# First stage of a four-layer convolution kernel: group norm by half-pair units with VectorE transposes in place of TensorE matmuls

## The chip, the cores and the metric

The kernel runs on one core of a Trainium2 chip. The metric is device time in microseconds (us) of one execution. Five engines work beside each other, each through its own fixed list of instructions: TensorE (PE in the profile, its weight loads PEld), VectorE (DVE), ScalarE (ACT), GpSimd (POOL) and SyncE (SP), which here only issues DMA transfers. ScalarE and GpSimd issue a few transfers too.

## What is computed

The input x has 8 images of 384 channels with 32 x 32 pixels. Four layers follow one another, each of the form x = x + layer(groupnorm(x)). Only the first matters here, and of it the part up to its batch norms:

```python
def _gn(v, G=32, eps=1e-5):
    g = v.reshape(B_, G, C_ // G, H_, W_)
    m = jnp.mean(g, axis=(2, 3, 4), keepdims=True)
    s = jnp.var(g, axis=(2, 3, 4), keepdims=True)
    return ((g - m) / jnp.sqrt(s + eps)).reshape(v.shape)

def _dwproj(x, dw, g, b, pw):          # for q, k and v
    y = lax.conv_general_dilated(x, dw, (1, 1), ((1, 1), (1, 1)), feature_group_count=C, ...)
    y = jax.nn.gelu(_bn(y, g, b), approximate=False)
    return jnp.einsum('oc,bchw->bohw', pw, y)

x = x + _L0_conv_ref(_gn(x), ...)      # q, k, v by _dwproj, attention in 8 heads, projection, batch norm
```

Each image is normalised over groups of 12 channels. Three depthwise 3 x 3 convolutions, for q, k and v, read the normalised image. Each result gets a batch norm, whose mean and variance run over all 8 images, then a gelu and a 384 x 384 product. So no result of the convolutions can be used until the statistics of all images are there: the convolved values go to device memory and are fetched again in the next stage.

## The kernel before, in words

The whole first stage is written out by hand: a manual schedule holds every engine to the order of the program text.

**Stacks.** The input was laid out on the host as `xs`. A stack puts the four image rows that two neighbouring output rows read on four neighbouring partitions (partition modulo 4 is the row offset d; d = 0 and 3 are rows of the neighbours, so each image row lies twice). A tile `xs` m holds half an image (two of its four channel sets g, three channel chunks c each, 512 columns per chunk) in 128 x 3072 values, loaded by four transfers of 384 KB (L281), one for each d. Before, `load_half` makes tile m of image m // 2, half m % 2. There are 16 tiles; eight are loaded at the start, the first four by SP and ScalarE together. Some tiles live in five image buffers that later stages use too, the others in a pool of six.

**Work.** Images are taken in pairs k = 0 to 3. Each pair has ten works: four of kind y (first chunk of q, k and v together), four of kind a (a later chunk of q and k), two of kind v (a later chunk of v). A work is a run of small matmuls (L545) into four PSUM banks, alternating between the `big` and the `mm` pool; then copies by ScalarE into a tile y (L555, two of 1024 columns or four of 512), four of 512-column statistics by VectorE (L561), and four stores by SP to device memory (L566, L571, L580; 128 or 256 KB each). The pool of y has four buffers. In the last pair VectorE also aggregates the statistics (L585).

**Norm.** `norm(k)` gives the steps that normalise pair k, and the table AT says at which work of pair k-1 each of them is put into the engines' order:
- `begin`, four times: VectorE takes statistics of a tile (six L334, two L337).
- `middle`: TensorE multiplies the means and variances by the group matrix `gs4` (L343, into bank `gpa`); VectorE copies (L348), subtracts (L351) and squares (L352).
- `end`: a second matmul by `gs4` (L358, `gpb`), VectorE adds (L360), GpSimd takes the power -0.5 (L98), VectorE makes the shift (L365).
- `apply`, four times: ScalarE scales and shifts 128 x 1536 values of each image (L379; for the second image of pair 0 VectorE does it, L377), and GpSimd zeroes the rows outside the image (four L382).

For pair 0 all of it stands ahead of the first work. For pairs 1 and 2 AT is (0, 0, 1, 2, 4, 5, 6, 7, 8, 9). The loads of later tiles are queued on SP between the stores, two or four parts per work.

**End of the stage.** Ahead of the last pair's stores SP moves the tile statistics of x (L486, eight small transfers). Ahead of the last-but-one work, `spread_qk` begins to spread q's and k's statistics, with two matmuls behind that work (L425); it borrows one y buffer. Behind that work's copies ScalarE applies the gelus of q and k of image 0 (L243). After the last work `spread_v` does the same for v with one matmul (L458, `pmovev`). Then the next stage begins on TensorE with the projection `pq` (L703).

Of the kernel before, what the change touches and what calls it, by code (L numbers as in the profile page):

```python
# [14 lines left out]
P = 128  # L15
# [40 lines left out]
def tile_kernel(ctx: ExitStack, tc: tile.TileContext, i: dict, out: bass.AP):  # L56
# [199 lines left out]
    with ExitStack() as pa:  # L256
# [8 lines left out]
        halves_of = {}  # L265
        IN_IM = (0, 1, 2, 3, 4, 11, 12)

        def load_half(m, queue):

            b, h = divmod(m, 2)  # L270
            t = (
                image(f"xs{m}") if m in IN_IM
                else xa.tile([P, KC, N], F32, tag="xs", name=f"xs{m}")
            )
            halves_of[m] = t.rearrange("p c n -> p (c n)").rearrange("p (k n) -> p k n", n=HALF)

            def part(d):
                w = KC * N
                s = W + (0 if d in (1, 2) else W if d == 3 else -W)
                src = i["xs"][s : s + B * C * N].rearrange("(b e m n) -> b e m n", b=B, e=2, m=32)  # L280
                queue[d].dma_start(  # L281
                    out=t.rearrange("p c n -> p (c n)")[d::4],
                    in_=src[b, 1 - d % 2, :, h * w : (h + 1) * w],
                )

            return [lambda d=d: part(d) for d in range(4)]

        for m in range(4):
            for f in load_half(m, (nc.sync, nc.sync, nc.scalar, nc.scalar)):
                f()  # L290
        gs4 = wa.tile([P, P], F32, name="gs4_sb")
        nc.gpsimd.dma_start(out=gs4, in_=i["gs4"])
# [5 lines left out]
        for m in range(4, 8):  # L298
            for f in load_half(m, 4 * (nc.sync,)):
                f()  # L300
        g4 = const.tile([P, P], F32, name="g4_sb")
        ident = const.tile([P, P], F32, name="ident_sb")
        sels = wa.tile([P, 3, P], F32, name="sels_sb")
        isv = wa.tile([P, 5], F32, name="isv_sb")
        msk = wa.tile([P, 28], F32, name="msk_sb")
# [12 lines left out]
        sv = wa.tile([P, KC - 1, 4, NK, 6], F32, name="sv")  # L318
        zy = wa.tile([P, 16, 2], F32, name="zy")
        zqk = wa.tile([P, KC - 1, 8, 2], F32, name="zqk")  # L320
        zv = wa.tile([P, KC - 1, 4, 2], F32, name="zv")
# [3 lines left out]
        def norm(k):  # L325

            state = {}
            mv = sa.tile([P, 2, 4, 2], F32, tag="gp_mv", name=f"gmv{k}")
            xt = [[halves_of[4 * k + 2 * j + h] for h in range(2)] for j in range(2)]

            def begin(j, h):
                for g in (2 * h, 2 * h + 1):
                    for c in range(KC):
                        nc.vector.bn_stats(  # L334
                            xst[:, g, 2 * k + j, c, :], xt[j][h][:, g % 2 * KC + c, :]
                        )
                    nc.vector.bn_aggr(  # L337
                        mv[:, j, g, :], xst[:, g, 2 * k + j].rearrange("p c s -> p (c s)")
                    )

            def middle():
                pg = bank(f"gpa{k}")
                nc.tensor.matmul(  # L343
                    pg[:, :16], lhsT=gs4, rhs=mv.rearrange("p j g s -> p (j g s)"),
                    start=True, stop=True,
                )
                ga = sa.tile([P, 8, 2], F32, tag="gp_ga", name=f"gga{k}")
                nc.vector.tensor_copy(ga.rearrange("p j s -> p (j s)"), pg[:, :16])  # L348
                dm = sa.tile([P, 8], F32, tag="gp_dm", name=f"gdm{k}")
                mvf = mv.rearrange("p j g s -> p (j g) s")  # L350
                nc.vector.tensor_tensor(dm, mvf[:, :, 0], ga[:, :, 0], ALU.subtract)  # L351
                nc.vector.tensor_tensor(dm, dm, dm, ALU.mult)  # L352
                state["ga"], state["dm"] = ga, dm

            def end():
                ga, dm = state["ga"], state["dm"]
                pb = bank(f"gpb{k}")
                nc.tensor.matmul(pb[:, :8], lhsT=gs4, rhs=dm, start=True, stop=True)  # L358
                ve = sa.tile([P, 8], F32, tag="gp_ve", name=f"gve{k}")
                nc.vector.scalar_tensor_tensor(  # L360
                    ve, pb[:, :8], 1e-5, ga[:, :, 1], ALU.add, ALU.add
                )
                ss = sa.tile([P, 2, 8], F32, tag="gp_ss", name=f"gss{k}")
                rsqrt(ss[:, 0, :], ve, 8)
                nc.vector.scalar_tensor_tensor(  # L365
                    ss[:, 1, :], ga[:, :, 0], -1.0, ss[:, 0, :], ALU.mult, ALU.mult
                )
                state["ss"] = ss

            def apply(g):  # L370
                ss, h = state["ss"], g // 2
                for j in range(2):
                    n = 4 * j + g
                    d = xt[j][h][:, g % 2 * KC : g % 2 * KC + KC, :]
                    sc, sh = ss[:, 0, n : n + 1], ss[:, 1, n : n + 1]
                    if k == 0 and j == 1:
# [9 lines left out]

            return (
                [lambda j=j, h=h: begin(j, h) for j in range(2) for h in range(2)]
                + [middle, end] + [lambda g=g: apply(g) for g in range(4)]
            )  # L390

        PLAN = ["y0 a01 y1 a11 y2 v1 y3 a02 a12 v2"] * last + [
            "y0 a01 y1 a11 y2 a02 y3 a12 v1 v2"
        ]
        work = [
            (k, w[0], int(w[1]), int(w[2:] or 0)) for k, p in enumerate(PLAN) for w in p.split()
        ]
        NW = len(work) // NK
        AT = (0, 0, 1, 2, 4, 5, 6, 7, 8, 9), (0, 3, 3, 4, 6, 7, 8, 8, 9, 9)
        steps = {}  # L400

        def spread_qk():
# [9 lines left out]
            for z, n, dst in zip(zs, nv, both):  # L412
                sq = sa.tile([P, ng], F32, tag="ssq", name=f"ssq{n}")
                nc.vector.tensor_tensor(sq, z[:, :, 0], z[:, :, 0], ALU.mult)
                nc.vector.tensor_tensor(z[:, :, 1], z[:, :, 1], sq, ALU.add)
                for s in range(2):
                    nc.vector.tensor_tensor(
                        dst[:, :, s], z[:, :, s].unsqueeze(1).to_broadcast([P, n, ng]),
                        isv[:, v0 : v0 + n].unsqueeze(2).to_broadcast([P, n, ng]), ALU.mult,
                    )  # L420
# [29 lines left out]

        def spread_v():

            m = zv.rearrange("p c g s -> p (c g) s")
            sq = sa.tile([P, 8], F32, tag="ssv", name="ssv")
            nc.vector.tensor_tensor(sq, m[:, :, 0], m[:, :, 0], ALU.mult)
            nc.vector.tensor_tensor(m[:, :, 1], m[:, :, 1], sq, ALU.add)
            pm = bank("pmovev")
            nc.tensor.matmul(  # L458
                pm[:, :16].rearrange("p (s x) -> p s x", s=2), lhsT=sels[:, 2, :],
                rhs=m.rearrange("p x s -> p s x"), start=True, stop=True,  # L460
            )
            got = sa.tile([P, 4, 4], F32, tag="gotv", name="gotv")
            nc.vector.tensor_tensor(
                got, pm[:, :16].rearrange("p (x g) -> p x g", g=4),
                msk[:, 24:].unsqueeze(1).to_broadcast([P, 4, 4]), ALU.mult,
# [3 lines left out]
            nc.vector.tensor_copy(fv[:, :, 1:], f.rearrange("p (s c) -> p s c", s=2))  # L469
# [25 lines left out]
        for n, (k, kind, s, c) in enumerate(work):  # L495
            at = n % NW
            if kind == "v":
                c = s
            if at == 0:
                for m in ((8, 9, 10, 11), (12,), (13, 14, 15), ())[k]:  # L500
                    loads += load_half(m, 4 * (nc.sync,))
                if k == 0:
                    load_late()
                steps = {}
                for a, f in zip(AT[k + 2 > last], norm(k + 1) if k < last else ()):
                    steps.setdefault(a, []).append(f)
            for _ in range(2 if k == 0 else 4):
                if loads and (k > 0 or at > 1):
                    loads.pop(0)()
            if k == last - 1 and at == 3:  # L510
                acts[0] = {v: image(f"g{v}_0") for v in (2, 1, 0)}
                for v, t in acts[0].items():
                    loads += fetch_raw(t, v, rqk[0], rv[:, 0])
            if k == last and at == 0:
# [3 lines left out]
            if k == last and at == 8:  # L518
# [5 lines left out]
            else:  # L524
                two = [big(f"pk{n}_{r}") for r in range(2)]
                banks = [two[r // 2][:, r % 2 * HALF : (r % 2 + 1) * HALF] for r in range(4)]
                outs = [(t, 2 * r, 2) for r, t in enumerate(two)]
            passes = [(j, x) for j in range(2 if kind == "v" else 1) for x in (1, 0, 2)]
            nq = 2 if kind == "y" else 4
            cols = [slice(P // nq * q, P // nq * (q + 1)) for q in range(nq)]  # L530
            for p in passes:
                j, x = p
                c0, c1 = max(0, 1 - x), W - max(0, x - 1)
                for q in range(nq):
                    if kind == "v":
                        g, w = q, slice(32 + 16 * j, 64 + 16 * j)
                    elif kind == "y":
                        g, j, w = s, q, slice(0, 64)
                    else:
                        (u, j), w = divmod(q, 2), slice(0, 32)  # L540
                        g = 2 * s + u
                    src = halves_of[4 * k + 2 * j + g // 2][:, g % 2 * KC + c, :]
                    src = src.rearrange("p (h w) -> p h w", w=W)
                    for r, rs in enumerate(quads):
                        nc.tensor.matmul(  # L545
                            banks[r][cols[q]].rearrange("p (h w) -> p h w", w=W)[:, :, c0:c1],
                            lhsT=cws[rs, c, g, x, w], rhs=src[rs, :, c0 + x - 1 : c1 + x - 1],
                            start=(p == passes[0]), stop=(p == passes[-1]),
                        )
            if k == last and at == 8:  # L550
# [3 lines left out]
            for src, r, w in outs:  # L554
                nc.scalar.copy(y[:, r : r + w, :].rearrange("p a n -> p (a n)"), src)  # L555
            st = (
                sy[:, 4 * s : 4 * s + 4] if kind == "y"
                else sv[:, c - 1] if kind == "v" else sqk[:, c - 1, s]
# [3 lines left out]
            for q in range(4):  # L562
                if kind == "y":
                    v, j = divmod(q, 2)
                    to = rqk[2 * k + j, c] if v == 0 else rv[c, 2 * k + j]
                    nc.sync.dma_start(  # L566
                        out=to[:, 4 * s : 4 * s + 4, :],
# [1574 lines left out]
```

## Time and profile before

| what | us |
| --- | --- |
| runs: median of 3 (lowest to highest) | 3538.39 (3537.48 to 3539.07) |
| the profiled execution's own time | 3538.58 |
| its span in the profile | 3536.8 |
| TensorE busy (share of the span) | 3386.1 (96%) |
| VectorE, ScalarE, GpSimd busy | 1686.8, 1294.6, 213.8 |
| first matmul of the convolutions L545 / first of the next stage L703 | 35.56 / 269.18 |
| matmuls of the convolutions L545, busy in all | 178.2 |
| VectorE statistics of the tiles L334, mean of one | 0.67 |
| VectorE statistics of y L561, mean of one | 0.68 |
| ScalarE applications L379, mean of one | 1.70 |

A row of the order of time has start, length, engine, line, operation, tile written <- tile read, shape, the count of instructions merged in it, and in brackets how long the engine was idle before and what ended the wait. A row of a stretch has its bounds and length, then busy time and instruction counts of PE, PEld, DVE, ACT and POOL, the granted TensorE clock (1.00 is full), the busy share of the 16 DMA engines and GB/s. The median of the runs and the profiled execution differ by 0.2 us.

### The profile page before, as it was taken

The numbers are of one execution on the slowest core, as the hardware profiler recorded it, in microseconds if no ns is written. First come the engines' busy times: TensorE is split into PE (matmuls) and PEld (weight loads), VectorE is DVE, ScalarE is ACT, GpSimd is POOL, SyncE is SP. The second block draws the span as 40 slices with busy tenths as digits, with TensorE's granted clock in tenths as the row PEclk, the third lists the DMA queues.
The fourth block names the chain that finished last, engine by engine and source line by source line (L and its number), as shares of the span: only waits on it lengthen the run. The fifth ranks groups of instructions, "written<-read, shape, count | busy, mean of one in ns | idle before, by whom it ended". The sixth has DMA issues, their size and how long they took to land.

```text
span 3536.8 us, 44871 instructions
## 1 busy us (share of the span) xinstructions
PE 3386.1 (96%) x18615; PEld 1459.1 (41%) x18615; DVE 1686.8 (48%) x2821; ACT 1294.6 (37%) x1512; POOL 213.8 (6%) x226
## 2 busy tenths in 40 slices
PE   5879999999999999998999999999999999999897
PEld 2333434343434343433344444444444444434434
DVE  6762232323232323234256475564755647556663
ACT  3554544444444444433212323223232232332222
POOL 2100000000000000000000100101001010010112
PEclk9999999999999999999999999999999999999898
DMA  8883212121212121121800010101101011010000
GB/s 301 245 256 85 58 35 71 35 70 38 66 45 60 49 57 56 49 58 58 307 22 21 35 45 28 54 21 35 51 26 51 21 35 57 35 39 18 0 31 24
DMA packets 86309, 234.16 MB, mean 66 GB/s; under 512 B 21688, under 2 KB 21912, under 8 KB 79178
## 3 DMA queue, kind: packets, MB, share of 16 engines
q1 hardware_dynamic: 83882, 222.75, 19.7%
q10 hardware_dynamic: 1248, 4.72, 0.3%
q0 software_dynamic: 960, 3.67, 0.3%
q8 instruction: 151, 2.47, 0.3%
q14 instruction: 68, 0.56, 0.0%
HBM read 145.91 MB, written 75.59 MB: 63 GB/s over the span
## 4 chain that ended last, share of the span: by engine, by line
PE 40%; DVE 9%; ACT 1%; DMA 1%; POOL 1%; issue 0%; DVEq 0%; ACTq 0%; POOLq 0%
PE y L1471 12%; PE ph L1450 9%; DVE y L1546 5%; PE pq L1591 4%; PE pw L1554 3%; PE pf L1898 3%; PE s L1769 2%; PE pav L1795 2%; DVE hd L1436 1%; PE pk L1744 1%; DMA o<-o 1%; PE pv L1753 1%; PE xsb L1730 1%; PE plog L1200 1%; PE pss L1808 1%; DVE off L1661 1%
## 5 line engine op out<-in xcount | busy, mean ns | idle before, releaser
L796 ACT ACTIVATE p<-s 128x1024 f32<-128x1024 f32 x512 | 496.6, 1021 | 365.7 <-PE s L789 365.1
L804 PE MATMUL pav<-p,vt 64*64 64x512 f32 x4096 | 494.1, 588 | 0.0
L1471 PE MATMUL y<-hd,w_sb 128*128 128x512 f32 x1080 | 488.6, 600 | 3.5 <-DVE hd L1436 3.5
L1450 PE MATMUL ph<-h,w_sb 128*128 128x512 f32 x1104 | 486.8, 595 | 4.4 <-ACT h L1399 4.3
L789 PE MATMUL s<-qk,qk 48*64 48x512 f32 x3072 | 370.3, 592 | 0.0
L1450 PEld LDWEIGHTS ph<-h,w_sb 128*128 128x128 f32 x1104 | 207.0, 190 | 265.6 <-issue 249.5
L1471 PEld LDWEIGHTS y<-hd,w_sb 128*128 128x128 f32 x1080 | 199.9, 191 | 248.1 <-issue 235.8
L804 PEld LDWEIGHTS pav<-p,vt 64*64 64x64 f32 x4096 | 167.1, 133 | 275.0 <-issue 273.9
L765 DVE COPY ta<-pav 128x512 f32<-128x512 f32 (+1 forms) x65 | 44.2, 682 | 474.9 <-PE pav L804 474.9
L1460 ACT ACTIVATE hd<-ph,b_sb 128x512 f32<-128x512 f32 x180 | 122.8, 682 | 312.3 <-PE ph L1450 312.3
L1546 DVE SCALAR_TENSOR_TENSOR y<-h,tap,y 128x961 f32<-128x961 f32 (+1 forms) x192 | 233.8, 1241 | 0.6
L1661 DVE SCALAR_TENSOR_TENSOR off<-q,dw_sb,off 128x225 f32<-128x225 f32 (+3 forms) x432 | 212.2, 548 | 1.6
L789 PEld LDWEIGHTS s<-qk,qk 48*64 48x64 f32 x3072 | 112.9, 133 | 221.3 <-issue 198.8
L545 PE MATMUL pk<-xs,cws_sb 32*32 32x496 f32 (+3 forms) x3840 | 178.2, 626 | 21.3 <-DVE gve L360 6.8
L81 DVE COPY qk<-pq 128x512 f32<-128x512 f32 x48 | 33.2, 691 | 261.1 <-PE pq L703 261.1
L1786 ACT ACTIVATE p<-s 128x1024 f32<-128x1024 f32 x96 | 96.1, 1023 | 166.5 <-PE s L1769 142.0
L1436 DVE TENSOR_TENSOR hd<-hd,cb 128x512 f32<-128x512 f32 x180 | 122.4, 685 | 41.0 <-ACT hd L1460 40.8
L1831 POOL TENSOR_TENSOR p<-p,p 128x1024 f32<-128x1024 f32 x48 | 113.0, 2355 | 349.8 <-ACT p L1786 349.7
L1554 PE MATMUL pw<-y,upw 128*128 128x512 f32 x288 | 129.8, 604 | 4.1 <-DVE y L1546 4.0
L703 PE MATMUL pq<-g,wq_sb 128*128 128x512 f32 x288 | 129.9, 601 | 0.0
L703 PE MATMUL pq<-g,wk_sb 128*128 128x512 f32 x288 | 129.2, 598 | 0.0
L1898 PE MATMUL pf<-att,wp_sb 128*128 128x512 f32 x288 | 127.6, 598 | 0.5 <-DVE x L1906 0.5
(316 smaller groups left out, 3641.8 us busy)
## 6 DMA issues: line engine op xcount, KB each, us to landing
rqk<-y SPq DMA_DIRECT2D x96, 256.0 KB
g<-rqk SPq DMA_DIRECT2D x96, 256.0 KB
xs<-in_xs_dram SPq DMA_DIRECT2D x56, 384.0 KB
g<-rv SPq DMA_DIRECT2D x48, 256.0 KB
xh<-in_x_dram SPq DMA_DIRECT2D x48, 256.0 KB
f<-in_x_dram SPq DMA_DIRECT2D x24, 512.0 KB
f<-o SPq DMA_DIRECT2D x24, 512.0 KB
o<-ot SPq DMA_DIRECT2D x42, 256.0 KB
```

The lines of the kernel that those rows point to most:

```text
L545: nc.tensor.matmul(banks[r][cols[q]].rearrange("p (h w) -> p h w", w=W)[:, :, c0:c1], lhsT=cws[rs, c, g, x, w], rhs=src[rs, :, c0 + x - 1 ...
L703: nc.tensor.matmul(pq, lhsT=w_in[v][:, c, pr * P : (pr + 1) * P], rhs=rows_of(acts[b][v][:, c, :], h * H // 2, (h + 1) * H // 2) if v == 0 ...
L789: nc.tensor.matmul(s[64 * k : 64 * k + 64, j * HALF : (j + 1) * HALF], lhsT=kt[r, k0 : k0 + 64], rhs=qt[r, h * HALF : (h + 1) * HALF], sta ...
L796: nc.scalar.activation(p, s, AF.Exp, scale=scale)
L804: nc.tensor.matmul(pav[k][64 * j : 64 * j + 64, :], lhsT=vts[b % 2][r, kc, 2 * hd : 2 * hd + 2, :].rearrange("p a b -> p (a b)"), rhs=p[r, ...
L1436: nc.vector.tensor_tensor(hd, hd, state["cb"], ALU.mult)
L1450: nc.tensor.matmul(ph, lhsT=w1[:, e, c, dc * P : (dc + 1) * P], rhs=state["h1"][c], start=(c == 0), stop=(c == KC - 1),)
L1471: nc.tensor.matmul(y, lhsT=w2[:, e, dc, m * P : (m + 1) * P], rhs=state[h, k], start=(k == 0), stop=(k == NE * KC - 1),)
L1546: nc.vector.scalar_tensor_tensor(d, f, tap2[:, c, t : t + 1], d, ALU.mult, ALU.add)
L1554: nc.tensor.matmul(pw[h], lhsT=upw2[:, c, m * P : (m + 1) * P], rhs=y[c][:, hs], start=(c == 0), stop=(c == KC - 1),)
L1661: nc.vector.scalar_tensor_tensor(d, f, dw3[:, t : t + 1], d, ALU.mult, ALU.add)
L1898: nc.tensor.matmul(pf[:, hs], lhsT=wp3[:, pr, m * P : (m + 1) * P], rhs=att[:, pr, hs], start=(pr == 0), stop=(pr == NPAIR3 - 1),)
```

## The change

The unit of the norm and of the order of work becomes half a pair: one tile of each of the two images, eight units u in all.

- Tile m is now pair m // 4, half m // 2 % 2, image m % 2 of the pair, so tiles 0 and 1 make the first unit.
- `norm(u)` has five steps: `begin` for each of the two tiles, `finish`, `apply` for two channel sets. They are put at works 0, 1, 2, 3 and 3 of the unit before. `finish` has no matmul: VectorE transposes means and variances in blocks of 32 x 32, so that what lay on partitions lies along columns, sums the owned rows, forms the variance, has GpSimd take the power, spreads the two results of each row over 16 columns and transposes back.
- The order of work in a unit is y0 a1 y1 a2 and a v set of its own half (v0). Unit 6 has no v set; unit 7 ends with that of unit 6 (v-1) and its own (v0). There are 40 works of the same kinds and counts as before; a set of v now holds both later chunks of one half in place of one chunk of both halves.
- Later tiles are loaded two parts per work, from the table LOADS; image 0 is fetched from unit 5.
- `gs4` and its load go; two small tiles `mvs` are filled with zeros on GpSimd ahead of the weights' loads. `spread_v` follows the new sets, with two more mask operations, and `sels`, `isv` and `msk` change their shapes.

In the engines' orders, `middle` and `end` go (20 VectorE instructions, 8 matmuls and 4 powers on GpSimd in all), and eight runs of `finish` come, each with ten VectorE instructions and a power on GpSimd. From `pq` on the orders of all engines are those of before.

The diff, cut to its core:

```diff
-            b, h = divmod(m, 2)
+            k, h, j = m // 4, m // 2 % 2, m % 2
...
-                    in_=src[b, 1 - d % 2, :, h * w : (h + 1) * w],
+                    in_=src[2 * k + j, 1 - d % 2, :, h * w : (h + 1) * w],
...
-        gs4 = wa.tile([P, P], F32, name="gs4_sb")
-        nc.gpsimd.dma_start(out=gs4, in_=i["gs4"])
+        mvs = [wa.tile([P, 2, 32], F32, name=f"mvs{t}") for t in range(2)]
+        for t in mvs:
+            nc.gpsimd.memset(t, 0.0)
...
-            def middle():
-                pg = bank(f"gpa{k}")
-                nc.tensor.matmul(
-                    pg[:, :16], lhsT=gs4, rhs=mv.rearrange("p j g s -> p (j g s)"),
...
-            def end():
-                ga, dm = state["ga"], state["dm"]
-                pb = bank(f"gpb{k}")
-                nc.tensor.matmul(pb[:, :8], lhsT=gs4, rhs=dm, start=True, stop=True)
...
+            def finish():
...
+                m8, v8, rs = small_[:, 0:2], small_[:, 2:4], small_[:, 4:6]
+                dm, var, wide = small_[:, 8:40], turned[:, 1, :], [P, 2, 16]
+                nc.vector.transpose(
+                    turned.rearrange("p t y -> p (t y)"), mv.rearrange("p t y -> p (t y)")
+                )
+                nc.vector.tensor_reduce(m8, owned(turned[:, 0, :]), AX.XY, ALU.add)
+                nc.vector.scalar_tensor_tensor(
+                    dm.rearrange("p (g y) -> p g y", g=2), m8.unsqueeze(2).to_broadcast(wide),
+                    -0.125, turned[:, 0, :].rearrange("p (g y) -> p g y", g=2),
+                    ALU.mult, ALU.add,
+                )
                 nc.vector.tensor_tensor(dm, dm, dm, ALU.mult)
...
+                nc.vector.tensor_tensor(dm, dm, var, ALU.add)
+                nc.vector.tensor_reduce(v8, owned(dm), AX.XY, ALU.add)
+                nc.vector.tensor_scalar(v8, v8, 0.125, 1e-5, ALU.mult, ALU.add)
+                rsqrt(rs, v8, 2)
+                nc.vector.tensor_copy(rows[:, 0], rs.unsqueeze(2).to_broadcast(wide))
                 nc.vector.scalar_tensor_tensor(
...
+                    rows[:, 1], m8.unsqueeze(2).to_broadcast(wide), -0.125, rows[:, 0],
+                    ALU.mult, ALU.mult,
+                )
+                nc.vector.transpose(
+                    ss.rearrange("p t y -> p (t y)"), rows.rearrange("p t g y -> p (t g y)")
+                )
...
-                    if k == 0 and j == 1:
+                    if u == 0 and j == 1:
                         nc.vector.tensor_scalar(d, d, sc, sh, ALU.mult, ALU.add)
...
-            return (
-                [lambda j=j, h=h: begin(j, h) for j in range(2) for h in range(2)]
-                + [middle, end] + [lambda g=g: apply(g) for g in range(4)]
-            )
-
-        PLAN = ["y0 a01 y1 a11 y2 v1 y3 a02 a12 v2"] * last + [
-            "y0 a01 y1 a11 y2 a02 y3 a12 v1 v2"
-        ]
...
-        AT = (0, 0, 1, 2, 4, 5, 6, 7, 8, 9), (0, 3, 3, 4, 6, 7, 8, 8, 9, 9)
+            return [
+                lambda: begin(0), lambda: begin(1), finish, lambda: apply(0), lambda: apply(1)
+            ]
+
+        NU0 = 2 * NK
+        work = []
+        for u in range(NU0):
+            order = "y0 a1 y1 a2" + " v0" * (u < NU0 - 2) + " v-1 v0" * (u == NU0 - 1)
+            work += [(u, w[0], int(w[1:])) for w in order.split()]
+        AT = {0: 0, 1: 1, 2: 2, 3: 3, 4: 3}
...
+        LOADS = {0: (8, 9, 10), 1: (11, 12), 3: (13,), 4: (14, 15)}
...
-                for m in ((8, 9, 10, 11), (12,), (13, 14, 15), ())[k]:
-                    loads += load_half(m, 4 * (nc.sync,))
+                for m in LOADS.get(u, ()):
+                    loads += load_tile(m, 4 * (nc.sync,))
...
-            for _ in range(2 if k == 0 else 4):
-                if loads and (k > 0 or at > 1):
+            for _ in range(2):
+                if loads and n > 2:
                     loads.pop(0)()
...
-            if k == last and at == 0:
+            if u == NU0 - 1 and at == 0:
                 x_moments()
...
                     if kind == "v":
-                        g, w = q, slice(32 + 16 * j, 64 + 16 * j)
+                        (g, c), w = divmod(q, 2), slice(32 + 16 * j, 64 + 16 * j)
+                        c += 1
...
-                    src = halves_of[4 * k + 2 * j + g // 2][:, g % 2 * KC + c, :]
+                    src = xs_of[4 * k + 2 * h + j][:, g * KC + c, :]
```

## The prediction

> **What bounds the kernel now.** I read the stretches first, then TensorE's order of time in the first stage, then the waits, then VectorE and ScalarE around one pair. The stretches (busy time of PE, PEld, DVE, ACT, POOL, then clock, DMA share, GB/s):
>
> ```profile
> 0.00:34.00 34.00, 1.20 (x4) 1.00 (x4) 19.12 (x42) 3.06 (x3) 4.79 (x11) 1.00 0.94 384
> 34.00:80.00 46.00, 35.96 (x645) 15.64 (x647) 33.24 (x64) 19.01 (x23) 13.61 (x28) 0.85 0.72 245
> 80.00:160.00 80.00, 64.22 (x1443) 28.07 (x1426) 52.88 (x98) 51.24 (x59) 11.40 (x31) 0.94 0.80 231
> 160.00:220.00 60.00, 42.08 (x911) 19.72 (x908) 39.40 (x75) 31.98 (x38) 6.84 (x17) 0.88 0.92 305
> 220.00:260.00 40.00, 37.23 (x867) 16.86 (x861) 28.44 (x93) 19.44 (x28) 1.70 (x2) 0.97 0.85 225
> 260.00:270.00 10.00, 3.12 (x50) 1.58 (x32) 6.93 (x44) 6.63 (x9) 0.00 (x0) 0.84 0.53 140
> 270.00:1680.00 1410.00, 1395.61 (x9464) 561.39 (x9462) 442.69 (x750) 659.45 (x675) 10.79 (x7) 1.00 0.20 55
> ```
>
> From 270 us TensorE is busy 1395.6 of 1410 us, in an order the change leaves alone. So what moves the first attention matmul (pq, at 269.18) moves the end by the same amount. Before it TensorE has only 178.2 us of convolution to do. Its order of time shows the rest as gaps:
>
> ```profile
> 28.15 0.61 PE L343 MATMUL gpa<-gmv,gs_sb 128*128 128x16 f32 x2 [28.15 <-DVE gmv L337]
> ...
> 35.56 15.82 PE L545 MATMUL pk<-xs,cws_sb 32*64 32x512 f32 x288 [5.54 <-POOL xs L382]
> 57.38 0.58 PE L343 MATMUL gpa<-gmv,gs_sb 128*128 128x16 f32 x2 [6.00 <-DVE gmv L337]
> 57.89 4.79 PE L545 MATMUL pk<-xs,cws_sb 32*64 32x512 f32 x48
> ...
> 119.56 0.58 PE L343 MATMUL gpa<-gmv,gs_sb 128*128 128x16 f32 x2 [11.40 <-DVE gmv L337]
> ...
> 188.09 0.58 PE L343 MATMUL gpa<-gmv,gs_sb 128*128 128x16 f32 x2 [11.06 <-DVE gmv L337]
> ...
> 268.77 0.58 PE L458 MATMUL pmovev<-zv,sels_sb 128*128 128x16 f32 x2 [6.88 <-DVE zv L456]
> ```
>
> 35.6 us pass before the first convolution. Then the norm matmul of the next pair, in TensorE's fixed order, waits 6.0, 11.4 and 11.1 us for VectorE's statistics. The waits agree (total, times, longest):
>
> ```profile
> PE gpa L343 <- DVE gmv L337: 28.4, 3, 11.4
> ACT y L555 <- DMA rqk<-y: 17.5, 3, 9.5
> ```
>
> Pair 1's statistics begin at 98.44, pair 2's at 157.69: 59.3 us per pair for some 40 of TensorE.
>
> VectorE and ScalarE give the prices:
>
> ```profile
> 98.44 1.86 DVE L334 BATCH_NORM_STATS2 xst<-xs 128x6 f32<-128x512 f32 x3
> ...
> 102.52 1.88 DVE L334 BATCH_NORM_STATS2 xst<-xs 128x6 f32<-128x512 f32 x3
> ...
> 106.59 2.41 DVE L561 BATCH_NORM_STATS2 sy<-y 128x6 f32<-128x512 f32 x4
> ...
> 80.49 1.94 ACT L555 COPY y<-pk 128x1024 f32<-128x1024 f32 x2
> 82.28 3.26 ACT L379 ACTIVATE xs<-xs,gss 128x1536 f32<-128x1536 f32 x2
> 85.41 2.07 ACT L555 COPY y<-pk 128x512 f32<-128x512 f32 x4
> ```
>
> Start to start: statistics of one tile 4.06 us on VectorE, of one result y 2.33; two applications 3.13 on ScalarE, a copy of y 1.8 or 1.9.
>
> **The start.** The first unit needs two tiles, not four. Tile 0 is ready at 9.6 and tile 1 at 14.8 (VectorE starts there now); its statistics end at 18.9 instead of 28.1. The rest of the norm now takes 28.1 to 32.2. The new finish: two transposes, two reductions, six small operations and a power on GpSimd. A transpose of 512 columns takes 702 ns and an 8-element operation 168, so 64 columns are about 0.24. Reductions of 64 to 96 elements take 0.22 to 0.25 (L442, L435), small ones step at 0.2. The power with its hops took 1.13 for 3 elements and 1.96 for 8, so about 0.97 for 2. Sum: 0.5 + 0.43 + 5 x 0.22 + 0.97 = 3.0 us (the small operation ahead of the power is in the 0.97). The operands are new in form: I bound it by 2.3 (each at the 0.17 floor, power 0.8) and 4.4 (each half as dear again), and take 3.0, nearest the rows. Scale at 21.9, then 3.34 us to the first convolution as now (32.22 to 35.56): 25.3, a gain of 10.3. Weights and row mask issued on GpSimd landed at 20.9 and 21.8; a 64 KB load before them goes and two small fills come, so they just fit.
>
> **A unit in the steady state.** Work is unchanged: 16 y, 16 a, 8 v, the same matmuls, copies, stores and statistics. TensorE no longer waits for norm matmuls. But each engine keeps a fixed order, and in it is a loop. VectorE: statistics of tile 1, y, tile 2, a, then finish: 4.06 + 2.33 + 4.06 + 2.33 + 3.0 = 15.8. All four applications now stand together on ScalarE, ahead of the copies of the second a and the v: 6.26 + 1.8 + 1.9 = 10.0. VectorE needs the v's statistics (1.3 after the copy) before the next unit's tiles: the loop is 27.1 us, 54.2 per pair against 59.3. Queued behind the wait for finish: those copies, their banks, so the next y on TensorE. TensorE (two y at 2.7, two a at 3.4, v at 7: 19.2), ScalarE (16) and VectorE's sum (23) fit inside. The last unit has no next norm.
>
> Costed at nothing: the v set per half (again 192 matmuls and four 256 KB stores, only the slices differ) and the new order of tile loads on SP. Two parts per work go out ahead of that work's stores, as in the first pair now. Tile 11 needs the buffer of tile 0, free after unit 0; the last, 15, is issued in unit 4 and read in unit 6. The cover is one loop, 27 us; without it a late tile costs the loop its transfer, about 5 us (9.6 to 14.8 for tile 1).
>
> [...] after the 6.0 us gap a y takes 4.79 instead of 2.7, with a granted clock of 0.85 over 34 to 80. The loop leaves TensorE some 8 us idle per unit, seven times instead of three. If all of that were on the path, 7 x 2.1 = 15 us would be lost and about 3 gained. The loop by the rows says it is covered: the next y on TensorE runs beside 4.06 us of tile statistics. I charge it only at the first and last unit.
>
> **The sum.** VectorE starts unit 0's loop at 24.1 (two applications of unit 0 are its own, 2.2 us). With the first y at 6.3 us (as 35.56 to 41.86) unit 0 takes 31.8: 55.9. Five units of 27.1: 191.4. Unit 6 adds two aggregations (1.3): scale at 208.5, first application done 211.6, TensorE starts unit 7 at 212.3. y 4.5, a 3.4, y 2.7, a 3.4, v 7: 233.4. The eight moment transfers hold SP for 7.3 us (222.65 to 229.93 now); they stand ahead of unit 7's stores. SP: stores of unit 6's last a to 220.5, moments to 227.8, y 230.4, a 233.9, landing 2.5 later: the copy of the last but one set, which needs that buffer, starts at 236.4. In the trace that copy starts at 254.58 and pq follows at 269.18: 14.6 (the gelus ahead of the last copy are the same), plus 0.4 for two mask operations. Pq at 251.4 against 269.2: 17.8 us, 10.3 of it at the start. The profiled execution took 3538.58 (span 3536.8 and 1.8 around), 0.2 from the median 3538.39. So 3520.8: 3521.
>
> **Rivals.**
> 1. Transfers become the bound (0.26). Busy DMA time to 270 us is 223.6 (shares above times lengths), 32.0 of it before 34. The change removes none. I need the rest at 0.86 to 0.88 of the time; 80 to 260 shows 0.85 on average, 0.92 in its densest part. At 0.85: 34 + 191.6 / 0.85 = 259.4, so 3529. For it: ScalarE's copies wait for stores 17.5 us. Against: half of these waits lie in the first pair, behind the burst of startup loads, and the loop asks for no more than five stores of y per 27 us. At 0.92 it would be 242.3, a floor of 3512; at the 0.94 of the startup loads 237.8: 3507.
> 2. A shorter loop (0.14): finish at 2.3 us gives 8 x 0.7 = 5.6 more: 3515.
> 3. The loop gains nothing (0.08 with the next): unit 30 us, only the start's gain: 3528 to 3531.
> 4. Slower: finish is eight times on the path. 17.8 us are gone at 2.2 us more each, that is when the two transposes and two strided reductions cost 0.78 each instead of 0.23. At the 1.65 of the present power on GpSimd: 8 x 5.7 - 17.8, 28 us slower: 3566. Against: 512 columns transpose in 0.70.
>
> **Numbers.** The loop as summed 0.52, transfers 0.26, shorter 0.14, the last two 0.08. Low 3507: transfers at their densest. High 3531: finish at 4.4 (8 x 1.4 = 11) or only the start. Measurement tells 0.2% (7 us) from no change: faster than 3531 0.90, within 0.07, slower 0.03.
>
> **What would show it.** First convolution near 25; finish near 3.0; no L343 matmul; begin of statistics every 27 us; ScalarE's four applications in one run of 6.3 just after each finish; pq near 251; from there the same as before. It is wrong if copies wait for DMA in units 1 to 6, or if the finish exceeds 4.4.

## The result, and the profile after

The changed kernel takes 3523.09 us (median of 6 runs, 3521.31 to 3526.03) against 3538.43 us (6 runs, 3536.58 to 3540.06). The ratio is 0.9958, with a 95% interval of 0.9945 to 0.9971: 15.3 us less. The forecast was 3521. The profiled execution, the fastest of the six, took 3521.31 us; its span is 3519.5.

First the stretches of the kernel after, with the columns as before:

```profile
0.00:34.00 34.00, 9.56 (x176) 4.84 (x184) 20.07 (x46) 7.91 (x9) 11.03 (x28) 1.00 0.94 382
34.00:80.00 46.00, 34.74 (x826) 17.16 (x815) 34.05 (x77) 28.73 (x34) 6.64 (x18) 0.92 0.95 334
80.00:160.00 80.00, 64.90 (x1427) 32.70 (x1412) 62.14 (x135) 45.06 (x52) 9.88 (x27) 0.88 0.88 274
160.00:220.00 60.00, 44.74 (x898) 22.54 (x906) 48.36 (x114) 35.18 (x43) 6.64 (x19) 0.82 0.86 249
...
270.00:1680.00 1410.00, 1393.94 (x9483) 561.27 (x9482) 446.37 (x765) 658.83 (x677) 3.90 (x4) 0.99 0.20 57
```

TensorE already works in the first 34 us. From 270 on nothing has changed: 1393.9 of 1410 us busy. So the gain has to lie ahead of pq, and TensorE's order of time shows it there:

```profile
24.44 11.94 PE L554 MATMUL pk<-xs,cws_sb 32*64 32x512 f32 x219 [24.44 <-POOL xs L387]
...
77.02 22.70 PE L554 MATMUL pk<-xs,cws_sb 32*64 32x512 f32 x480 [7.20 <-POOL xs L387]
...
132.40 16.95 PE L554 MATMUL pk<-xs,cws_sb 32*64 32x512 f32 x337 [4.06 <-POOL xs L387]
...
187.84 14.62 PE L554 MATMUL pk<-xs,cws_sb 32*64 32x512 f32 x288 [5.84 <-POOL xs L387]
211.88 21.39 PE L554 MATMUL pk<-xs,cws_sb 32*64 32x512 f32 x480 [9.42 <-POOL xs L387]
...
252.12 0.61 PE L464 MATMUL pmovev<-bothv,sels_sb 128*128 128x32 f32 x2 [7.45 <-DVE bothv L454]
252.54 7.47 PE L705 MATMUL pq<-g,wq_sb 128*128 128x512 f32 x12
```

The first convolution starts at 24.44 instead of 35.56, pq at 252.54 instead of 269.18: 16.6 us, while the span is 17.3 shorter. The three waits for norm matmuls are gone. In their place TensorE waits at the start of most units, now for normalised data (GpSimd's row zeroing is the last step of the application). Three kinds of wait tell who holds whom (total, times, longest; the first total has the 24.4 us of the startup in it, the other four waits are 4.1 to 9.4):

```profile
PE pk L554 <- POOL xs L387: 51.0, 5, 24.4
ACT xs L384 <- DVE gss L372: 47.3, 7, 8.2
DVE sy L571 <- ACT y L565: 2.4, 1, 2.4
```

ScalarE waits for the scale in each of the seven units, 6.8 us on average. VectorE waits once, in unit 0, for the copy of a unit's first y: the tile statistics cover TensorE's late start, as forecast (in unit 2 that copy starts at 83.16, and VectorE comes to it at 85.77). No copy of y waits for a store. The loop itself, on VectorE, unit 1 to 2 (the L338 rows are statistics of tiles, L571 those of y, a and v):

```profile
66.57 0.23 DVE L353 STREAM_TRANSPOSE gt<-mvs 128x64 f32<-128x64 f32 x1
66.83 0.17 DVE L356 TENSOR_REDUCE gs<-gt 128x2 f32<-128x16 f32 x1
...
68.97 0.18 DVE L367 COPY gr<-gs 128x32 f32<-128x32 f32 x1 [0.87 <-POOL gs L98]
...
69.41 0.24 DVE L372 STREAM_TRANSPOSE gss<-gr 128x64 f32<-128x64 f32 x1
69.58 2.43 DVE L571 BATCH_NORM_STATS2 sy<-y 128x6 f32<-128x512 f32 x4
76.96 2.47 DVE L571 BATCH_NORM_STATS2 sqk<-y 128x6 f32<-128x512 f32 x4 [4.95 <-ACT y L565]
79.35 2.46 DVE L571 BATCH_NORM_STATS2 sv<-y 128x6 f32<-128x512 f32 x4
```

and between the two on ScalarE:

```profile
69.69 6.34 ACT L384 ACTIVATE xs<-xs,gss 128x1536 f32<-128x1536 f32 x4 [8.11 <-DVE gss L372]
75.94 3.84 ACT L565 COPY y<-pk 128x1024 f32<-128x1024 f32 x6
```

The finish takes 3.1 us (66.57 to 69.7). Then four applications in a row, then the copies of the second a and of the v, and only then can VectorE go on, after 4.95 us idle. Tile statistics of the next unit begin at 81.72.

### The profile page after: what moved, and what is told of

Same layout as the page of the kernel before. It is cut to its first block, busy times and chain, and to the rows that moved or that the text cites. A ratio compares the mean times of both kernels' runs of the same rounds, so it can differ in the third digit from the quotient of the medians.

```text
span 3519.5 us, 44915 instructions
## 1 busy us (share of the span) xinstructions
PE 3379.2 (96%) x18599; PEld 1468.1 (42%) x18599; DVE 1695.2 (48%) x2881; ACT 1298.0 (37%) x1514; POOL 211.3 (6%) x231
## 4 chain that ended last, share of the span: by engine, by line
PE 41%; DVE 9%; DMA 1%; ACT 1%; POOL 0%; issue 0%; DVEq 0%; ACTq 0%; POOLq 0%; SPq 0%
PE y L1473 12%; PE ph L1452 9%; DVE y L1548 5%; PE pq L1593 4%; PE pw L1556 3%; PE pf L1900 3%; PE s L1771 2%; PE pav L1797 2%; DVE hd L1438 1%; DMA o<-o 1%; PE pk L1746 1%; PE pv L1755 1%; PE xsb L1732 1%; PE pss L1810 1%; PE plog L1202 1%; DVE off L1663 1%
## 5 line engine op out<-in xcount | busy, mean ns | idle before, releaser
L554 PEld LDWEIGHTS pk<-xs,cws_sb 32*32 32x32 f32 (+1 forms) x3840 | 89.7, 116 | 150.4 <-issue 64.3
```

The costliest lines, as they stand in the source:

```text
L554: nc.tensor.matmul(banks[r][cols[q]].rearrange("p (h w) -> p h w", w=W)[:, :, c0:c1], lhsT=cws[rs, c, 2 * h + g, x, w], rhs=src[rs, :, c0 ...
```

## The experiments

My theory: this loop sets the pace of the first stage. Rivals: transfers are the bound; the sum of VectorE's or TensorE's work is; or the order of the work brings the gain and the norm's form little. Each ratio is to the kernel before on the same chip (medians of 3538.2 to 3539.0 us there), with its 95% interval. Differences from the kernel after are between medians, and a few us of them can be chance: the runs of one changed kernel spread over 4 to 6 us.

**Is the finish on the path?** Ten more two-element operations in each finish, multiplications by 1.

```diff
                 nc.vector.tensor_scalar(v8, v8, 0.125, 1e-5, ALU.mult, ALU.add)
+                for _ in range(10):
+                    nc.vector.tensor_scalar(v8, v8, 1.0, None, ALU.mult)
                 rsqrt(rs, v8, 2)
```

> The kernel after with ten more dependent two-element VectorE operations (multiplication by 1) in each finish, ahead of the power. Theory of the loop: 10 x 0.2 = 2.0 us, eight times on the path, 16 us: 3539, as slow as before. Rival, transfers or ScalarE are the bound and the finish has slack: at most 5 us, 3523 to 3528.

Measured 3538.83 us, ratio 0.9999 (0.9990 to 1.0007): 15.7 above the kernel after, and as slow as before. In the profile the first convolution is 2.26 later (26.70) and pq 16.0 later (268.57). Two microseconds in the finish, eight times, cost sixteen. That is the loop, without slack, and it is about the point at which rival 4 of the prediction said the gain would be gone (2.2 us per finish).

**Can the applications leave the loop?** The second application of each unit is held back until after the v set.

```diff
-        steps = {}
+        steps, late = {}, []
...
-                steps = {}
+                steps = {0: late}
+                late = []
                 for t, f in enumerate(norm(u + 1) if u + 1 < NU0 else ()):
-                    steps.setdefault(AT[t], []).append(f)
+                    if t == 4:
+                        late = [f]
+                    else:
+                        steps.setdefault(AT[t], []).append(f)
```

> The kernel after, with the second application of each unit moved behind the v set, to the start of the next unit. Theory of the loop (statistics, finish, applications, copies, statistics, 27.7 us per unit in the profile after): two of four applications, 3.1 us, leave the loop; six units of it lie ahead of the last two, so pq comes 19 to 21 us earlier, near 233, and the time is about 3503. Rival, transfers are the bound: at a DMA share of 0.90 to 0.92 after the startup loads pq cannot come before 242 to 247, so 3511 to 3516, with copies waiting for stores. Rival, VectorE's or TensorE's sum is the bound: no change, 3523.

Measured 3509.38 us, ratio 0.9915 (0.9898 to 0.9931): faster than the kernel after, though by 14 us and not 20. On ScalarE the four applications are now two and two:

```profile
69.24 3.23 ACT L384 ACTIVATE xs<-xs,gss 128x1536 f32<-128x1536 f32 x2 [5.50 <-DVE gss L372]
72.38 3.85 ACT L569 COPY y<-pk 128x1024 f32<-128x1024 f32 x6
76.08 3.26 ACT L384 ACTIVATE xs<-xs,gss 128x1536 f32<-128x1536 f32 x2
```

Tile statistics begin at 53.38, 78.16, 102.51 and 127.30: 24.4 to 24.8 us apart, 3.1 less than in the kernel after, as the theory wants. Unit 0 gained only 0.4 (VectorE waits 2.27 us there for the copy of its v), so five loops, not six, bring 16.0 us up to unit 6 (176.50 against 192.53). Pq starts at 236.03, 16.5 earlier, ahead of what the rival of the transfers allowed. Another 3 us, in the profiled execution, were lost at the very end of the program; see the last section.

**Which part of the change brings the gain?** First the half units with the norm of before: two matmuls per unit, at the place of the finish.

```diff
...
             def finish():
...
+                pg = bank(f"gpa{u}")
+                nc.tensor.matmul(pg[:, :8], lhsT=gs4, rhs=mv[:, :, :4], start=True, stop=True)
...
+                pb = bank(f"gpb{u}")
+                nc.tensor.matmul(pb[:, :4], lhsT=gs4, rhs=dm, start=True, stop=True)
```

> Half-pair units kept, but the norm by two TensorE matmuls per unit as before, put at the same place as the finish. Theory: TensorE's fixed order holds the second y of the unit back until VectorE's statistics are there, so the y starts cold about 15 us into the unit, its copy stands ahead of the four applications, and the loop grows from 27.7 to about 33.5 us: 7 x 5.8 = 41 us, 3563, slower than the kernel before. Rival: the matmuls cost only themselves (1.2 us) and one more us of finish: 8 x 1 to 2 us, 3531 to 3539.

Measured 3557.07 us, ratio 1.0051 (1.0034 to 1.0068): slower than before. TensorE's order of time:

```profile
70.73 0.57 PE L348 MATMUL gpa<-mvs,gs_sb 128*128 128x8 f32 x2 [7.71 <-DVE mvs L341]
73.51 0.56 PE L354 MATMUL gpb<-gs,gs_sb 128*128 128x4 f32 x2 [2.21 <-DVE gs L352]
74.00 21.51 PE L539 MATMUL pk<-xs,cws_sb 32*64 32x512 f32 x480
103.13 0.56 PE L348 MATMUL gpa<-mvs,gs_sb 128*128 128x8 f32 x2 [7.62 <-DVE mvs L341]
```

The loop is 32.3 to 32.7 us (33.5 expected), the granted clock was 0.78 from 34 to 80 us and 0.80 to 0.85 from 80 to 260, and two matmuls that take 1.1 us hold the convolutions behind them for 10. So the half units lose with the norm of before in the place of the finish. The kernel before has a work of convolutions between its two matmuls, and there the second waits 0 to 0.4 us behind the first pair; here it waits 2.2 in each unit. Without that the run might come near the kernel before (7 x 2.2, an estimate of 15 us); such an order was not run.

**And the other half of it:** the transposes in the kernel before, with its pairs, its order and its startup.

```diff
...
-            return (
-                [lambda j=j, h=h: begin(j, h) for j in range(2) for h in range(2)]
-                + [middle, end] + [lambda g=g: apply(g) for g in range(4)]
-            )
+            return (
+                [lambda j=j, h=h: begin(j, h) for j in range(2) for h in range(2)]
+                + [finish] + [lambda g=g: apply(g) for g in range(4)]
+            )
...
-        AT = (0, 0, 1, 2, 4, 5, 6, 7, 8, 9), (0, 3, 3, 4, 6, 7, 8, 8, 9, 9)
+        AT = (0, 0, 1, 2, 4, 6, 7, 8, 9), (0, 3, 3, 4, 6, 8, 8, 9, 9)
```

> The kernel before with its pairs, its order of work and its startup, but the norm by the transposes and row sums in place of the two matmuls per pair. Theory: the waits of TensorE for statistics (6.0, 11.4, 11.1 us) fall away; VectorE's loop per pair is then 28.7 us to the scale, four times an application pair and a copy on ScalarE (20 us) and 1.3: 50 us in place of 59.3. Three pairs: 28 us less by the loop, one more at the start; transfers at a share of 0.90 to 0.93 allow pq at 240 to 247, so 3510 to 3517. Rival, the half units make the gain and the transposes only the finish shorter: 3530 to 3537.

Measured 3513.91 us, ratio 0.9929 (0.9913 to 0.9946): 9.2 us faster than the whole change. Its start is close to that of before (34.12 against 35.56), and its pairs are faster than two half units:

```profile
34.12 18.41 PE L550 MATMUL pk<-xs,cws_sb 32*64 32x512 f32 x344 [34.12 <-POOL xs L387]
...
243.65 8.43 PE L708 MATMUL pq<-g,wq_sb 128*128 128x512 f32 x12
```

The tile statistics within pairs 1 and 2 begin at 84.52 and 134.28, 49.8 us apart (50 expected), against 59.3 before and 55.4 for two units of the kernel after: here each application stands between two copies. And now transfers do hold the copies (ScalarE's waits, 34 to 240 us):

```profile
ACT y L560 <- DMA rqk<-y: 18.7, 8, 4.9
ACT y L560 <- DMA rv<-y: 16.0, 4, 6.3
```

**The place of the finish.** The kernel after with the finish one work earlier, ahead of the statistics of the first a.

```diff
-        AT = {0: 0, 1: 1, 2: 2, 3: 3, 4: 3}
+        AT = {0: 0, 1: 1, 2: 1, 3: 3, 4: 3}
```

> The kernel after, with the finish put one work earlier, right behind the second tile's statistics and ahead of those of the a. Theory of the loop: one set of y statistics (2.33 us) leaves the stretch ahead of the finish and falls into VectorE's wait for the copies (4.5 to 5.0 us per unit): the loop falls from 27.7 to 25.4, pq comes 7 x 2.33 = 16 us earlier, near 236: 3507. Rival, transfers: with a share near 0.93 pq at about 242, 3512 to 3513. Rival, VectorE's sum is the bound: no change.

Measured 3508.99 us, ratio 0.9913 (0.9896 to 0.9929), 14 us below the kernel after through one number in a table. The copy behind the power comes at 66.23, 91.95, 117.24, 142.95 and 168.24: a loop of 25.3 to 25.7. Unit 7 starts 14.2 us earlier (197.73), pq 13.4 earlier (239.15): less than 16, because unit 0 gained 1.4 only and the tail took a little more.

**Both together.** The same line and the late second application.

> Early finish and late second application together. The loop alone would be 22.3, less than VectorE's own sum (two tiles 8.1, five sets 11.7, finish 3.1: 22.9), so VectorE would be busy throughout: 1.6 us per unit below the late application alone, six or seven units, 10 us: pq near 226, 3498 to 3500. Rival, transfers: that would need a DMA share of 1.0 between 34 us and pq; at the 0.93 to 0.95 of the densest stretches pq stays at 234 to 240, so 3505 to 3511, with copies waiting for stores.

Measured 3505.96 us, ratio 0.9907 (0.9890 to 0.9923): the lowest median here, 17 us below the change, yet only 3 below either part, and the runs overlap (3503.45 to 3508.60, against 3505.65 to 3509.48 with the early finish alone). VectorE is now the bound in the middle: the copy behind the power comes at 66.93, 89.97 and 113.00, 23.0 apart, which is its own sum of 22.9. But the end of the stage gives it back: unit 7 starts at 187.63, 24 us ahead of the kernel after, and pq at 235.68, only 17 ahead. The waits of ScalarE that the kernel after did not have:

```profile
ACT y L569 <- DMA rv<-y: 11.4, 5, 3.3
ACT y L569 <- DMA rqk<-y: 9.1, 4, 3.6
```

12.9 of these 20.5 us lie behind 170 us. The DMA share is 0.95 from 34 to 80 us, 0.93 from 80 to 160. What the rival of the transfers said of this kernel came: pq, time and waiting copies, at 3506 and not at the 3529 where the prediction feared it. But the eight moment transfers share in it: SP issues them from 205.67 to 212.38, ahead of the stores of unit 7, and at 217.79 VectorE has waited 4.81 us for the store of a buffer that the spread of q's and k's statistics borrows (see the next experiment). Which of the two holds the end was not tested: neither less traffic nor late moments were tried with both edits.

**The tail.** The eight moment transfers of x behind the stores of the last unit's second a.

```diff
-            if u == NU0 - 1 and at == 0:
+            if u == NU0 - 1 and at == 4:
                 x_moments()
```

> The kernel after, with the eight small moment transfers of x put behind the stores of the last unit's second a, not ahead of its first store. Theory of the tail: they hold SP 7.8 us (220.5 to 228.5 in the profile after), the copy of the last-but-one set waits for the buffer whose store stands behind them, until 237.7, while TensorE has its matmuls done by about 233: 4 to 5 us, 3518 to 3519. Rival: the copy waits for something else (the spread of q's and k's statistics): within 1 us of 3523.

Measured 3523.40 us, ratio 0.9960 (0.9947 to 0.9974): no difference from the kernel after that the runs could show (3519.40 to 3525.17). The theory had the wait of that copy wrong. First the kernel after, then the late moments:

```profile
234.91 0.33 DVE L454 TENSOR_TENSOR room<-zy,isv_sb 128x48 f32<-128x48 f32 x2 [3.91 <-DMA rqk<-y]
237.53 0.16 DVE L479 TENSOR_TENSOR ss<-fqk 128x3 f32<-128x3 f32 x1
237.72 1.93 ACT L565 COPY y<-pk 128x1024 f32<-128x1024 f32 x2 [8.65 <-DVE ss L479]
```

```profile
232.08 0.33 DVE L454 TENSOR_TENSOR room<-zy,isv_sb 128x48 f32<-128x48 f32 x2 [0.23 <-DMA rqk<-y]
236.00 0.16 DVE L479 TENSOR_TENSOR ss<-fqk 128x3 f32<-128x3 f32 x1
236.18 1.93 ACT L565 COPY y<-pk 128x1024 f32<-128x1024 f32 x2 [6.26 <-issue]
```

The copy of the last-but-one set starts 0.18 or 0.19 us behind the start of L479, the step right behind VectorE's last read of `room`, the borrowed buffer. It does so in both kernels and in all eight experiments (the line number differs in some). So it waits for the spread of q's and k's statistics, the cause that the rival named. The moments act on it through `room`: VectorE waited 3.91 us for the store of that buffer, which stands behind them, and with late moments 0.23. The next limit is close: the spread's matmuls stand behind the last-but-one set in TensorE's order, which is done at 234.1, and VectorE's part follows. So, counted from the start of unit 7, the copy comes 2.4 us earlier (236.18 - 212.73 against 237.72 - 211.88), not 4 to 5. VectorE then waits 2.55 us for the moments that land late, ahead of the last set's statistics; pmovev gains 2.0, less than the runs' spread. With the late application:

> Late second application and late moment transfers together. By the loop and the tail both gains hold: 14 us and 4 us, 3504 to 3506. If the transfers are the bound by now (share 0.93 to 0.95 up to 160 us with the late application), the tail gives less than half: 3507 to 3510.

Measured 3507.87 us, ratio 0.9911 (0.9896 to 0.9927), 1.5 below the late application alone, which is within the spread of either (3503.48 to 3509.37, and 3505.96 to 3511.89 for the late application alone).

## Why the prediction was right

- **Start.** Forecast 10.3 us, measured 11.1. The finish was forecast at 3.0 us: 3.1. From scale to first convolution I carried over 3.34 us; it took 2.6 (21.81 to 24.44). The 0.7 is one row operation of GpSimd, the second, behind which TensorE starts: 1.06 us before, beside VectorE's application (32.22 to 36.33), and 0.34 now, where VectorE's two parts end at 23.88 and that operation starts at 24.05.
- **Loop.** Forecast 27.1, measured 27.5 to 27.9 (tile statistics at 53.81, 81.72, 109.19, 137.09). The parts: statistics 12.8, finish 3.1, applications 6.25, close to the forecast. The mis-sized term is the end: I took the two copies (3.7) and 1.3 behind them. VectorE has the statistics of a and v to do one after the other, 4.76 us, behind the first piece of the first copy (0.6 or 1.0): 5.4 to 5.8 in place of 5.0.
- **Clock.** TensorE idled 4 to 9 us at the start of most units and the granted clock was 0.82 to 0.92 between 34 and 220, but VectorE's tile statistics covered the slow y, as the rows said. Had the restarts lain on the path, they would have cost 15 us by the prediction's estimate (seven times the 2.1 us by which a y ran longer after the 6.0 us gap in the kernel before, 4.79 against 2.7). The finish has no slack (sixteen for two), the y has.
- **Unit 7, in part by luck.** Forecast 212.3, measured 211.88, but as a sum of misses that cancel: the next unit's tile statistics begin 2.1 us early at 53.81 (unit 0's first y was taken at 6.3 us, and its copy starts 4.9 behind the first matmul), five loops take 138.7 in place of 135.5, and from there unit 7 comes 1.5 sooner than forecast (19.4 in place of 20.9).
- **Tail.** The copy of the last-but-one set: 236.4 forecast, 237.72 measured; pq 251.4 and 252.54. The reason given for that copy, a buffer whose store stands behind the moments, was wrong in its last step: the copy waits for the spread of q's and k's statistics, and it is the spread's borrowed buffer whose store the moments delay. Of the 14.8 us from that copy to pq, the gelus with the table load ahead of them take 8.2.
- **The end.** Pq is 16.6 us earlier and the profiled span 17.3 shorter, so the gain passed through the rest nearly unchanged.
- **What the prediction did not see.** It priced the change as a whole. Of its two halves, the transposes alone are worth 25 us (3513.91), the half units with matmuls in the place of the finish cost 18 (3557.07), and together they give 15. Half units win 11 us at the start, but as ordered put all four applications between finish and copies. The early finish was there to be read in the loop of the prediction: VectorE waits between finish and copies (4.5 to 5.0 us in each unit, as measured), and statistics of 2.33 could have been moved into that wait.

## What to carry to other kernels

Where every engine keeps a fixed order, look for the loop that goes through several of them and add up its terms; the busiest engine is not the bound while such a loop is longer than its sum. A small matmul in TensorE's order costs the wait for its operand, because everything behind it waits too (1.1 us of work, 10 us of waiting here). Ask of a wait what ends it: a copy that seemed to wait for a store waited for the statistics. Shorten a loop by moving off it what its next step does not need (applications behind copies, statistics behind the finish), until an engine's sum or the transfers take over.

## What the runs showed of the hardware

**The same matmuls of TensorE, after the same wait, took a different time in two runs.** With pq 16.5 us earlier, the late application still led by 16.0 after 3 ms of unchanged work, and lost 3 us of it in the last 150. The same matmuls after the same wait of 4.23 us, first in the kernel after, then with the late application:

```profile
3407.74 3.36 PE L1797 MATMUL pav<-p,vt 128*64 128x512 f32 x8 [4.23 <-DVE tu L1845]
3410.91 1.90 PE L1810 MATMUL pss<-p,ones 128*64 128x512 f32 x6
```

```profile
3391.77 3.68 PE L1801 MATMUL pav<-p,vt 128*64 128x512 f32 x8 [4.23 <-DVE tu L1849]
3395.20 3.05 PE L1814 MATMUL pss<-p,ones 128*64 128x512 f32 x6
```

Six matmuls take 1.90 or 3.05 us, the eight ahead of them 3.36 or 3.68. The granted clock was 0.79 from 3405 to 3413 us in the first, and 0.66 from 3389 to 3399 in the second. The lead falls here from 15.97 to 14.55 us (the next matmuls start at 3412.74 and 3398.19). After two more long waits (7.68 us in both, then 4.11 and 3.88) it is 13.35 (L1746 at 3457.35, L1750 at 3444.00); there the granted clock was 0.76 from 3434 to 3448, and 0.62 from 3420 to 3434. What makes the clocks differ, no run here tests. This bounds what a single profile can tell: such differences, about 1.4 us at this place, lie within the runs' spread of 4 to 6 us.

**A row operation of GpSimd was slower beside VectorE's applications.** In the first application the zeroing of 128 x 96 values took 0.53 us once and 1.06 twice while VectorE scaled and shifted its tile parts, and 0.34 to 0.35 after them, in the kernel before. VectorE's parts took 1.07 to 1.10 us there and in the kernel after. What the two share, no run shows.

**Small VectorE operations of different kinds took much the same time.** In the finish they step, start to start, by 0.20 to 0.26 us: the transposes of 64 columns took 0.19 to 0.25 us, the strided reductions 0.17, the others 0.17 to 0.19. The estimate from a 512-column transpose (0.70) and an 8-element operation (0.17) was within 0.05 for the 64 columns.
